# First FFN of a macaron block: the order of its first five row tiles written out for all engines

## The chip, the cores and the metric

The kernel runs on one core of one Trainium2 chip. The metric is the device time of one execution in microseconds; the time before is a median of three runs. The engines are PE (TensorE: matmuls, and PEld for its weight loads), DVE (VectorE), ACT (ScalarE), POOL (GpSimd) and SP (SyncE, here only a queue that issues DMA transfers). Each engine takes its own instructions in order, and semaphores make it wait for the others.

## What is computed

One macaron layer on 2048 rows of 1024 numbers, in float32: half a feed-forward step (FFN), an attention step, half the same FFN again. The FFN is a binary-weight product with eight routed scales:

```python
# reference, cut
xf = x.reshape(-1, H)
routing = softmax(xf @ gate_w.T, axis=1)              # 8 experts
in_scale = routing @ in_channel_scale
out_scale = routing @ out_channel_scale
ffn = xf * in_scale @ sign(weight).T * out_scale + bias
...
x = x + 0.5 * ffn(layernorm(x))
x = x + attn(layernorm(x))        # convolution, 16 heads in blocks of 128, two projections
x = x + 0.5 * ffn(layernorm(x))
```

## The kernel before

The rows are cut into 16 tiles of 128. The program has four stages: the first FFN (to about 198 us of the profiled execution), the convolution, attention, and the second FFN. The change touches the first FFN, and the shared class `Ffn` and function `normalize` that the second also uses.

One tile t of the FFN passes these steps, each a method of `Ffn`. `norm` (line 184) takes the row's mean and variance on DVE (two `bn_stats`, line 155, and line 159), the reciprocal root on POOL (162) and applies them, on ACT (170) or, with `on_vector`, on DVE (166). `transpose` (193) turns the result with eight PE transposes into `xnT`, copied out in two halves. `gate` (203) makes the logits of eight experts, `route` (218) their softmax (the exponential on ACT, the rest on DVE), as a high and a low float32r part; `turn` (236) transposes it. `scale` (243) multiplies the small tables by it: the input scale multiplies `xnT` on DVE (261), the product is cast to float32r `yh` (263, on ACT or DVE) and the rest `yl` is found by POOL (264). `out_scale` (267) makes `osc`, through ACT. `main` (278) is the product of the two terms with the signs `sw`: eight chunks c of the inner dimension, two column halves h, two terms, 32 matmuls of 128x512 a tile (286). Then DVE multiplies a half by `osc` (295) and adds it to the row in place (296). `add_bias` (190) adds half the bias to the row by an accumulating DMA on POOL's queue.

After the FFN, `norm_x2` and `transpose_x2` (388, 395, called as `after` and `between`) store the row, normalise it for the attention step, transpose it into a window and, every third tile, run a transform on DVE (434 to 440).

PSUM has four kinds of banks of two each: `mm` (main products), `acc`, `tr`, `sm`. Rows live in a ring of eight buffers (`xring`), the raw weight rows in six others (`cwp`).

What sets the order: the framework keeps a dependency for each buffer and orders the instructions of each engine by a planner's estimates. Inside `with tc.manual_schedule()` (line 671) it keeps the written order. There stands `begin` (596), which loads the rows and weights, makes the constants and brings tiles 0 and 1 to their products, with the sign steps `sign(c)` on ACT between, and ends with tile 0's product:

```python
        ffn.norm(0)
        ffn.norm(1, on_vector=True)
        ffn.transpose(0)
        ffn.transpose(1, nc.vector.tensor_copy)
...
        def third():
            ffn.transpose(2, nc.vector.tensor_copy)
            ffn.norm(3, on_vector=True)
            ffn.add_bias(3)

        ffn.main(0, 0, 1, between=third)
```

Everything behind is ordered by the planner, along `run` (319), where iteration t holds gate t+2, scale t+1, the first half of product t with route t+2 in its middle, transpose t+3, `between` t-2, norm and bias t+4, the second half with turn t+2 in its middle, and `after` t-1. `pin` and `keep_in_program_order` hold single instructions in program order; the five loads of convolution and attention constants (673) are such, on POOL's queue.

Of the kernel before, what the change touches and what calls it, by code (L numbers as in the profile page):

```python
# [9 lines left out]
F32 = mybir.dt.float32  # L10
F32R = mybir.dt.float32r
DRAM = bass.MemoryType.DRAM
AF = mybir.ActivationFunctionType
# [4 lines left out]
P = 128  # L18
# [6 lines left out]
def kernel(  # L25
# [102 lines left out]
    def table_loads(tmp):  # L128

        raw = tmp[:, 0, 0:NB]  # L130
        for n, src in enumerate((ics, ocs)):
            for h in range(NH2):
                nc.gpsimd.dma_start(
                    out=raw[ts(2 * n + h, QC), :],
                    in_=src[:, ts(h, NB)].unsqueeze(0).broadcast_to([4, E, NB]),
                )
        return raw
# [13 lines left out]
    def normalize(dst, src, name, pinned=False, on_vector=False):  # L151

        stats = small.tile([P, NH2, 6], F32, name=f"st_{name}", tag="stats")
        for h in range(NH2):
            ins = nc.vector.bn_stats(out=stats[:, h, :], in_=src[:, ts(h, NB)])  # L155
            if pinned:
                pin(ins)
        mv = small.tile([P, 2], F32, name=f"mv_{name}", tag="mv")
        nc.vector.bn_aggr(out=mv, in_=stats)
        rstd = small.tile([P, 1], F32, name=f"rs_{name}", tag="rstd")  # L160
        nc.vector.tensor_scalar(rstd, mv[:, 1:2], EPS, None, ALU.add)
        nc.gpsimd.tensor_tensor(rstd, rstd, nhalf, ALU.pow)
        if on_vector:
            for h in range(on_vector):
                cols = ts(h, D // on_vector)
                nc.vector.tensor_scalar(dst[:, cols], src[:, cols], mv[:, 0:1], rstd, ALU.subtract, ALU.mult)
            return
        shift = small.tile([P, 1], F32, name=f"sh_{name}", tag="shift")
        nc.gpsimd.tensor_scalar(shift, mv[:, 0:1], rstd, -1.0, ALU.mult, ALU.mult)
        nc.scalar.activation(dst, src, AF.Identity, bias=shift, scale=rstd)  # L170

    class Ffn:
# [6 lines left out]
        def __init__(self, name, sw, work, xnp, first, end, row, ahead, after, between, beside):  # L179
            self.name, self.sw, self.work, self.xnp, self.first, self.end = name, sw, work, xnp, first, end  # L180
            self.row, self.ahead, self.after, self.between, self.beside = row, ahead, after, between, beside
            self.xns, self.xnTs, self.lgps, self.routs, self.rTs, self.oscs, self.ys = ({} for _ in range(7))

        def norm(self, t, pinned=False, on_vector=False):
            for n in range(t, min(t + 2, self.end)):
                self.ahead(n)
            self.xns[t] = self.xnp.tile([P, D], F32, name=f"xn_{self.name}_{t}", tag="xn")
            normalize(self.xns[t], self.row(t), f"{self.name}_{t}", pinned, on_vector)
# [4 lines left out]
        def transpose(self, t, copy=nc.scalar.copy):  # L193
            xn = self.xns.pop(t)
            xnT = self.work.tile([P, DC, P], F32, name=f"xnT_{self.name}_{t}", tag="xnT", bufs=3)
            for h in range(DC // 4):
                tr = bank("tr", [P, 4, P], f"tr_{self.name}_{t}_{h}")
                for c in range(4):
                    nc.tensor.transpose(tr[:, c, :], xn[:, ts(4 * h + c, P)], ident)  # L199
                copy(xnT[:, 4 * h : 4 * h + 4, :], tr)  # L200
            self.xnTs[t] = xnT
# [41 lines left out]
        def scale(self, t, copy=nc.scalar.copy, out=False):  # L243

            xnT, rT = self.xnTs.pop(t), self.rTs[t]
            yhl = self.work.tile([P, 2, DC, P], F32R, name=f"y_{self.name}_{t}", tag="y")
            scs = [bank("tr", [P, 4, P], f"is_{self.name}_{t}_{h}") for h in range(NH2)]
            for c in range(4):
                for h, sc in enumerate(scs):
                    nc.tensor.matmul(  # L250
                        sc[:, c, :],
                        lhsT=tables[ts(h, QC), ts(c, P)],
                        rhs=rT[ts(h, QC), :],
                        start=True,
                        stop=True,
                    )
            if out:
                self.out_scale(t)
            for h, sc in enumerate(scs):
                y = xnT[:, 4 * h : 4 * h + 4, :]  # L260
                nc.vector.tensor_tensor(y, y, sc, ALU.mult)
                yh, yl = (yhl[:, n, 4 * h : 4 * h + 4, :] for n in range(2))
                copy(yh, y)  # L263
                nc.gpsimd.tensor_tensor(yl, y, yh.bitcast(F32), ALU.subtract)  # L264
            self.ys[t] = yhl
# [12 lines left out]
        def main(self, t, *halves, between=None, at=DC - 2):  # L278
            y, osc, xrow = self.ys[t], self.oscs[t], self.row(t)
            pms = {h: bank("mm", [P, NB], f"pm_{self.name}_{t}_{h}") for h in halves}  # L280
            for c in range(DC):
                if between and c == at:
                    between()
                for h, pm in pms.items():
                    for n in range(2):
                        nc.tensor.matmul(  # L286
                            pm,
                            lhsT=y[:, n, c, :],
                            rhs=self.sw[:, c, ts(h, NB)],
                            start=(c == 0 and n == 0),  # L290
                            stop=(c == DC - 1 and n == 1),
                        )
            for h, pm in pms.items():
                o, xt = osc[:, ts(h, NB)], xrow[:, ts(h, NB)]
                nc.vector.tensor_tensor(pm, pm, o, ALU.mult)  # L295
                nc.vector.tensor_tensor(xt, xt, pm, ALU.add)  # L296
            if NH2 - 1 in pms:
                del self.ys[t], self.oscs[t]

        def fill(self):  # L300
# [8 lines left out]
                lambda: self.scale(a, out=True),  # L309
# [9 lines left out]
        def run(self):  # L319

            for t in range(self.first, self.end):
                self.on(self.gate, t + 2)
                if t + 1 in self.ys:
                    self.out_scale(t + 1)
                elif t + 1 < self.end:
                    self.scale(t + 1, out=True)
                route, turn = (lambda stage=stage: self.on(stage, t + 2) for stage in (self.route, self.turn))
                begun = t not in self.ys  # L330
                if begun:
                    route()
                else:
                    self.main(t, 0, between=route, at=DC // 2)
                self.on(self.transpose, t + 3)
                self.on(self.between, t - 2)
                self.on(self.norm, t + 4, t == self.first)
                self.on(self.add_bias, t + 4)
                if begun:
                    turn()  # L340
                else:
                    self.main(t, 1, between=turn, at=DC // 2)
                self.on(self.after, t - 1)
                self.beside(t)
# [251 lines left out]
    def begin(ffn, work):  # L596
# [5 lines left out]
        def load_raw(c):  # L602
            raws[c] = cwp.tile([P, D], F32, name=f"raw_{c}", tag="cw")
            nc.sync.dma_start(out=raws[c], in_=weight_t[ts(c, P), :])
# [13 lines left out]
        load_x(1)  # L618
        for c in range(6):
            load_raw(c)  # L620
        load_x(2)
        raw = table_loads(tmp)
# [5 lines left out]
        ffn.norm(0)  # L628
        ffn.norm(1, on_vector=True)
        ffn.transpose(0)  # L630
        ffn.transpose(1, nc.vector.tensor_copy)
        for h in range(NH2):
            hb = bank("acc", [P, NB], f"hb_{h}")
            nc.tensor.matmul(hb, lhsT=halves, rhs=brow[:, ts(h, NB)], start=True, stop=True)
            nc.vector.tensor_copy(hbias[:, ts(h, NB)], hb)
        ffn.add_bias(0)
        ffn.add_bias(1)
        ffn.gate(0)
        nc.scalar.copy(upper, raw)
        ffn.route(0)  # L640
        table_terms(raw, upper)
        ffn.gate(1)
        sign(0)
        load_raw(6)
        ffn.turn(0)
        ffn.route(1)
        sign(1)
        load_raw(7)
        load_x(3)
        ffn.scale(0)  # L650
        ffn.turn(1)
        sign(2, 3)
        ffn.scale(1, nc.vector.tensor_copy)
        sign(4, 5)
        ffn.norm(2, on_vector=True)
        ffn.add_bias(2)
        sign(6)
        ffn.out_scale(0)
        sign(7)

        def third():
            ffn.transpose(2, nc.vector.tensor_copy)
            ffn.norm(3, on_vector=True)
            ffn.add_bias(3)

        ffn.main(0, 0, 1, between=third)

    with ExitStack() as ph:
# [6 lines left out]
        ffn.run()  # L675
# [267 lines left out]
    ffn.run()  # L943
# [56 lines left out]
```

## Time and profile before

| | |
|---|---|
| median of three runs | 997.54 us (995.36 to 998.24) |
| the profiled execution's own time | 995.0 us |
| its span, first to last instruction | 992.9 us |
| PE busy in the span | 957.5 us, 96% |
| DVE, ACT, POOL busy | 653.7, 407.7, 256.4 us |
| first FFN: last addition to a row | starts at 198.1 us |
| first matmul of the convolution | 207.0 us |

Times in views are microseconds from the span's start. In a row of a timeline there stand the start, the length, the engine, the line, the operation, what it writes and reads, and how often it ran in a row; a bracket tells how long the engine was idle before it and what released it. Ends of matmuls are modelled, and records of neighbouring instructions overlap a little, so the distance from start to start is the better price of one. The granted clock is TensorE's, 1.00 for full speed.

### The profile page before, as it was taken

How to read it: one execution, taken by the hardware profiler on the slowest of the kernel's cores; microseconds unless marked ns; L12 is line 12 of the kernel's file. 1: busy time of each engine (PE TensorE's matmuls, PEld its weight loads, DVE VectorE, ACT ScalarE, POOL GpSimd, SP SyncE). 2: the span in 40 equal slices, each digit the busy share in tenths (PEclk: the TensorE clock that was granted, in tenths of full speed). 3: DMA queues.
4: the chain of work that ended last, by engine and by line, in shares of the span. 5: the costliest groups of instructions: out<-in, count | busy, mean ns of one | idle time of the engine just before them, and what ended most of it. 6: DMA issues, size and time to landing. Idle time of an engine off the chain costs nothing.

```text
span 992.9 us, 13803 instructions
## 1 busy us (share of the span) xinstructions
PE 957.5 (96%) x5036; PEld 622.8 (63%) x5036; DVE 653.7 (66%) x1231; ACT 407.7 (41%) x1113; POOL 256.4 (26%) x327
## 2 busy tenths in 40 slices
PE   5999999979999999999999999999999999899997
PEld 4778888746666666655555455545554556677776
DVE  5878887798795665637656465546555656777664
ACT  4476765401011111125546244536442653545440
POOL 4455543310011111003313120212022312534321
PEclk8999999989999999999999999999999999999999
DMA  9766554698787764326030430053004217655421
GB/s 271 208 180 195 157 171 153 229 362 300 279 257 178 202 174 123 96 101 228 18 111 1 168 109 1 0 196 102 1 1 170 44 36 209 161 162 158 110 79 64
DMA packets 37252, 143.08 MB, mean 144 GB/s; under 512 B 4345, under 2 KB 5369, under 8 KB 34754
## 3 DMA queue, kind: packets, MB, share of 16 engines
q1 hardware_dynamic: 27616, 101.35, 28.0%
q0 software_dynamic: 8544, 29.64, 15.7%
q10 hardware_dynamic: 1026, 11.22, 2.9%
q8 instruction: 40, 0.66, 0.3%
q14 instruction: 26, 0.21, 0.1%
HBM read 84.37 MB, written 41.04 MB: 126 GB/s over the span
## 4 chain that ended last, share of the span: by engine, by line
PE 47%; issue 26%; DVE 11%; DMA 7%; POOL 6%; ACT 1%; SPq 0%; POOLq 0%; DVEq 0%; ACTq 0%
PE pm_f L286 18%; PE cv L515 16%; POOL xr L774 3%; PE tr_f L199 2%; PE pp L908 2%; DMA xl<-win 2%; POOL p L830 2%; PE acc L889 1%; PE lgp_f L207 1%; PE is_f L250 1%; DVE st_f L155 1%; DMA g<-in_conv_w_dram 1%; PE pq L797 1%; DMA pw_sb<-in_proj_w_dram 1%; DMA xf<-x 1%
## 5 line engine op out<-in xcount | busy, mean ns | idle before, releaser
L286 PE MATMUL pm_f<-sw,y_f 128*128 128x512 f32 x1024 | 266.6, 408 | 0.2 <-DVE x L296 0.2
L286 PEld LDWEIGHTS pm_f<-sw,y_f 128*128 128x128 f32 x1024 | 186.8, 191 | 40.9 <-DVE x L296 0.4
L515 PE MATMUL cv<-v,u 128*128 128x342 f32 x576 | 166.3, 450 | 1.1 <-DVE u L506 1.1
L515 PEld LDWEIGHTS cv<-v,u 128*128 128x128 f32 x576 | 109.0, 189 | 58.2 <-ACT m L521 1.6
L830 POOL TENSOR_SCALAR_AFFINE_SELECT p<-p 128x512 f32<-128x512 f32 x64 | 40.0, 654 | 285.9 <-ACT p L828 285.9
L843 ACT ACTIVATE p<-p,anm 128x128 f32<-128x128 f32 x256 | 99.0, 388 | 17.5 <-DVE anm L840 17.5
L264 POOL TENSOR_TENSOR y_f<-xnT_f,y_f 128x512 fp32r<-128x512 f32 x64 | 81.3, 1288 | 70.0 <-ACT y_f L263 69.2
L521 ACT ACTIVATE m<-cv 128x342 f32<-128x342 f32 x42 | 19.0, 456 | 165.8 <-PE cv L515 148.6
L828 ACT COPY p<-sc 128x512 f32<-128x512 f32 x64 | 34.3, 587 | 111.2 <-PE sc L818 111.1
L840 DVE TENSOR_REDUCE anm<-p 128x4 f32<-128x512 f32 x64 | 40.9, 681 | 49.9 <-POOL p L830 49.9
L889 PE MATMUL acc<-oT,wo_sb 128*128 128x512 f32 x128 | 66.9, 615 | 0.5 <-DVE oT L881 0.5
L515 PE MATMUL cv<-v,g 128*128 128x342 f32 x192 | 56.9, 459 | 4.7 <-DVE v L440 4.7
L295 DVE TENSOR_TENSOR pm_f<-pm_f,os_f 128x512 f32<-128x512 f32 x64 | 44.3, 692 | 25.8 <-PE pm_f L286 25.6
L797 PE MATMUL pq<-qkv,wq_sb 128*128 128x512 f32 x128 | 61.0, 596 | 0.0
L797 PE MATMUL pq<-qkv,wk_sb 128*128 128x512 f32 x128 | 60.1, 592 | 0.0
L908 PE MATMUL pp<-pw_sb,o2T 128*128 128x512 f32 x128 | 57.6, 600 | 0.5 <-DVE xr L916 0.3
L781 PE MATMUL pv<-wv_sb,qkv 128*128 128x512 f32 x128 | 56.1, 592 | 0.0
L515 PEld LDWEIGHTS cv<-v,g 128*128 128x128 f32 x192 | 37.0, 194 | 24.3 <-DVE v L440 4.9
L506 DVE SCALAR_TENSOR_TENSOR u<-g,u 128x1024 f32<-128x1024 f32 x18 | 22.0, 1223 | 40.3 <-issue 30.7
L200 ACT COPY xnT_f<-tr_f 128x512 f32<-128x512 f32 x60 | 32.5, 589 | 37.7 <-PE tr_f L199 37.7
L843 ACT ACTIVATION_READ_ACCUMULATOR p<-p,anm 128x1 f32 x256 | 47.9, 187 | 0.0
L851 DVE TENSOR_TENSOR p<-p,asum 128x512 f32<-128x512 f32 x64 | 45.6, 712 | 2.2
(143 smaller groups left out, 1482.4 us busy)
## 6 DMA issues: line engine op xcount, KB each, us to landing
g<-in_conv_w_dram SPq DMA_DIRECT2D x28, 512.0 KB, 5.3
u<-in_conv_w_dram POOLq DMA_DIRECT2D x24, 512.0 KB, 6.3
xl<-win ACTq DMA_DIRECT2D x7, 1560.0 KB, 10.9
win<-xw SPq DMA_DIRECT2D x6, 1560.0 KB, 6.0
x<-in_x_dram SPq DMA_DIRECT2D x16, 512.0 KB, 4.6
raw<-in_weight_t_dram SPq DMA_DIRECT2D x16, 512.0 KB, 6.9
x<-hbias POOLq DMA_DIRECT2D x16, 512.0 KB, 5.8
x<-x SPq DMA_DIRECT2D x16, 512.0 KB, 5.2
```

Source lines behind the costliest of these rows:

```text
L264: nc.gpsimd.tensor_tensor(yl, y, yh.bitcast(F32), ALU.subtract)
L286: nc.tensor.matmul(pm, lhsT=y[:, n, c, :], rhs=self.sw[:, c, ts(h, NB)], start=(c == 0 and n == 0), stop=(c == DC - 1 and n == 1),)
L295: nc.vector.tensor_tensor(pm, pm, o, ALU.mult)
L515: nc.tensor.matmul(acc, lhsT=uk[:, c, :], rhs=V[k][:, c, :], start=(c == 0), stop=(c == DC - 1))
L781: nc.tensor.matmul(pv, lhsT=qkvs[g][2][:, c, ts(b, P)], rhs=wv_sb[:, c, ts(half, NB)], start=(c == 0), stop=(c == WC - 1),)
L797: nc.tensor.matmul(pq, lhsT=w_sb[:, c, ts(hp, P)], rhs=qkvs[g][n][:, c, :], start=(c == 0), stop=(c == WC - 1),)
L830: nc.gpsimd.affine_select(out=p, in_=p, pattern=[[0, BPG], [-1, P]], compare_op=ALU.is_ge, fill=NEG_INF, base=0, channel_multiplier=1,)
L840: nc.vector.tensor_reduce(nmax, p, AX.X, ALU.max, negate=True)
L843: nc.scalar.activation(p[:, b, :], p[:, b, :], AF.Exp, bias=nmax[:, b : b + 1], accum_out=asum[:, b : b + 1],)
L851: nc.vector.tensor_tensor(p, p, asum.unsqueeze(2).broadcast_to([P, BPG, P]), ALU.mult)
L889: nc.tensor.matmul(accs[g][m], lhsT=wo_sb[:, hp, ts(m, P)], rhs=oT, start=(hp == 0), stop=(hp == NHP - 1),)
L908: nc.tensor.matmul(pp, lhsT=o2T[:, m, ts(b, P)], rhs=pw_sb[:, m, ts(h, NB)], start=(m == 0), stop=(m == WC - 1),)
```

## The change

The written order now covers the first five tiles with all engines, and `run` begins at tile 5. In particular:

- The table loads go through ACT's DMA queue instead of POOL's, ahead of the weight rows in the written order.
- Weight rows 6 and 7 go to two buffers of the row ring and are asked for directly behind the others.
- `normalize` is cut into a class `Norm` with separate steps; tiles 0 and 1 are normalised by DVE in halves, tiles 2 and 3 by ACT.
- The bias copies move from DVE to ACT and ahead of the first norm; the tables' conversion on ACT (`upper`) too.
- `scale` is cut into `in_scale`, `multiply`, `split`, `out_scale`; in the written part casts and low terms are assigned to engines piece by piece, with the eight sign steps in between.
- `main` takes a table `beside` of steps to be written before matmul pair (c, h), and evicts a half directly after its last matmul; `apart` tells from which c the halves go one after the other.

```diff
@@ table_loads
-                nc.gpsimd.dma_start(
+                nc.scalar.dma_start(
@@ Norm
+        def by_vector(self, parts, which):
+            for h in which:
+                cols = ts(h, D // parts)
+                nc.vector.tensor_scalar(
+                    self.dst[:, cols], self.src[:, cols], self.mv[:, 0:1], self.rstd, ALU.subtract, ALU.mult
+                )
...
@@ Ffn
+        def split(self, t, h, copy=nc.scalar.copy, low=nc.gpsimd):
+            y = self.xnTs[t][:, 4 * h : 4 * h + 4, :]
+            yh, yl = self.y_terms(t, h)
+            copy(yh, y)
+            low.tensor_tensor(yl, y, yh.bitcast(F32), ALU.subtract)
...
+        def main(self, t, *halves, beside=None, apart=DC):
...
+            turns = [(c, h) for c in range(apart) for h in pms] + [(c, h) for h in pms for c in range(apart, DC)]
+            for c, h in turns:
+                beside.pop((c, h), lambda: None)()
...
@@ run
-                self.on(self.norm, t + 4, t == self.first)
+                self.on(self.norm, t + 4)
@@ begin
+            pl, tag = (cwp, "cw") if c < 6 else (xring, "x1")
...
         load_x(1)
+        raw = table_loads(tmp)
         for c in range(6):
             load_raw(c)
         load_x(2)
-        raw = table_loads(tmp)
+        load_raw(6)
+        load_raw(7)
+        load_x(3)
...
+            nc.scalar.copy(hbias[:, ts(h, NB)], hb)
+        nc.scalar.copy(upper, raw)
+        norms = [Norm(*ffn.begin_norm(t)) for t in range(2)]
+        norms[0].sums(0)
+        norms[0].sums(1)
+        norms[0].factor()
+        norms[1].sums(0)
+        for h in range(NH2):
+            norms[0].by_vector(2, (h,))
+            ffn.transpose(0, h)
+        norms[1].sums(1)
+        norms[1].factor()
+        ffn.gate(0)
+        table_terms(raw, upper)
+        norms[1].by_vector(2, (0, 1))
+        sign(0)
+        ffn.route(0)
+        ffn.transpose(1, 0)
+        sign(1)
+        ffn.transpose(1, 1, copy=nc.vector.tensor_copy)
+        ffn.turn(0)
         ffn.add_bias(0)
+        ffn.in_scale(0, "acc")
         ffn.gate(1)
+        ffn.multiply(0, 0)
+        sign(2)
+        ffn.split(0, 0, low=nc.vector)
+        ffn.multiply(0, 1)
+        ffn.split(0, 1)
         ffn.route(1)
+        sign(3, 4)
+        def scale_both():
+            ffn.out_scale(0)
+            ffn.in_scale(1)
+            ffn.multiply(1, 0)
+            sign(5)
+            ffn.split(1, 0, nc.vector.tensor_copy)
+            ffn.multiply(1, 1)
+            sign(6, 7)
+            ffn.split(1, 1, nc.vector.tensor_copy)
+            ffn.add_bias(1)
+        def next_rows():
+            ffn.out_scale(1)
+            ffn.norm(2)
+            ffn.add_bias(2)
+        def begin_third():
+            ffn.transpose(2)
+            ffn.norm(3)
+            ffn.add_bias(3)
+        ffn.main(
+            0, 0, 1,
+            beside={(2, 0): then((ffn.turn, 1)), (3, 0): scale_both, (5, 0): next_rows, (7, 1): begin_third},
+            apart=DC - 2,
+        )
+        ffn.main(1, 0, beside={(3, 0): then((ffn.gate, 2)), (6, 0): then((ffn.route, 2))})
+        ffn.transpose(3)
+        ffn.main(
+            1, 1,
+            beside={
+                (1, 1): then((ffn.turn, 2)),
+                (3, 1): then((ffn.scale, 2), (norm, 4), (plus, 4)),
+                (5, 1): then((ffn.gate, 3)),
+                (7, 1): then((ffn.route, 3)),
+            },
+        )
+        ffn.main(2, 0, beside={(2, 0): then((ffn.turn, 3), (ffn.after, 0)), (5, 0): then((ffn.scale, 3))})
...
+        ffn.after(3)
@@ after begin
-        ffn.run()
+        ffn.run(5)
@@ second FFN
-    ffn.run()
+    ffn.run(0)
```

In the part left out of `begin`, tiles 2 to 4 go on in the same manner: norms 5 to 8, gates and routes to 6, scales to 5, transposes to 7, `after` 0 to 3 and `between` 0 to 2 stand beside their products. The five constant loads on POOL's queue still stand behind `begin`.

## The prediction

> **What bounds the kernel now.** I read the page's head and slices first, then the busy time by stage, then the timelines of the engines over the first 90 us, because the change touches only the first feed-forward block (FFN) and mainly its first five row tiles.
>
> ```profile
> span 992.9 us, 13803 instructions
> PE 957.5 (96%) x5036; PEld 622.8 (63%) x5036; DVE 653.7 (66%) x1231; ACT 407.7 (41%) x1113; POOL 256.4 (26%) x327
> PE   5999999979999999999999999999999999899997
> PEclk8999999989999999999999999999999999999999
> ```
>
> PE is busy 96% of the span. The first slice (24.8 us) is at 5 tenths: that is the place where PE time is lost that this change can reach. To see how much, I cut the first 116 us at the starts of the tiles' main products (windows; columns: length, then busy time and count for PE, PEld, DVE, ACT, POOL, then PE clock, DMA share, GB/s).
>
> ```profile
> 0.00:22.00 22.00, 11.79 (x84) 8.53 (x84) 12.21 (x33) 9.37 (x17) 8.27 (x22) 0.85 0.91 274
> 22.00:35.70 13.70, 12.62 (x70) 9.67 (x68) 10.52 (x20) 8.06 (x13) 7.10 (x9) 0.87 0.95 311
> 35.70:49.35 13.65, 13.49 (x97) 9.87 (x97) 12.21 (x34) 6.83 (x16) 7.60 (x12) 0.87 0.54 118
> 49.35:84.00 34.65, 33.11 (x234) 26.39 (x232) 27.76 (x65) 24.11 (x51) 19.21 (x28) 1.00 0.61 167
> 84.00:116.40 32.40, 32.40 (x234) 26.41 (x232) 27.49 (x64) 21.96 (x47) 16.20 (x24) 1.00 0.65 197
> ```
>
> The last row is the settled loop: three tiles in 32.4 us, 10.8 us each, PE never idle. So the loss is 22.0 us ahead of tile 0's products, then tiles of 13.6, 13.6 and 13.0 us. The landmark for everything below is the start of tile 5's products, from where old and new code are the same. PE's timeline gives the starts of tiles 0, 1, 2 and 5:
>
> ```profile
> 22.07 7.37 PE L286 MATMUL pm_f<-sw,y_f 128*128 128x512 f32 x24
> 35.71 3.91 PE L286 MATMUL pm_f<-sw,y_f 128*128 128x512 f32 x9 [0.17 <-DVE x L296]
> 49.35 2.12 PE L286 MATMUL pm_f<-sw,y_f 128*128 128x512 f32 x8
> 83.94 2.11 PE L286 MATMUL pm_f<-sw,y_f 128*128 128x512 f32 x8
> ```
>
> In the second row 9 matmuls take 3.91 us, 0.43 each; in the settled chain of waits 32 take 2.04+1.95+1.83+1.85 = 7.67 us, 0.24 each. The clock by the microsecond says why:
>
> ```profile
> 24.00:25.00 1.00, 1.00 (x4) 0.50 0.97 361
> 25.00:26.00 1.00, 1.00 (x4) 0.72 1.02 418
> 35.00:36.00 1.00, 0.82 (x6) 0.90 0.09 20
> 36.00:37.00 1.00, 1.00 (x3) 0.50 1.03 197
> ```
>
> PE started its first products at half clock and fell back to it at 35.9, after 3.6 us (32.1 to 35.7) without a main product.
>
> **The change, part by part.** I walk the new order with durations of these timelines, each instruction starting when its engine and its inputs are free, 0.1 us per hand-over. Unit rows at half clock: four transposes 0.91 (16 in 3.65), a gate 1.08, a main matmul 0.43; at full clock 0.44, 0.57, 0.24.
>
> *Up to tile 0's gate.* Old: gate at 14.01, because PE first did both tiles' transposes (to 12.1) and the two bias products (12.10 to 14.0), which now run at 3.8 to 5.7, where PE is idle. New: statistics 4.5 to 5.75 (old 4.36; I add 0.15 for the table loads beside them), reciprocal root to 6.85, two half normalisations by DVE of 0.45 (half of 0.81), 6.95 to 7.85, transposes 7.5 to 9.3, the second ACT copy to 10.0, gate at 10.1. ACT must first convert the tables (0.62), and all its later copies queue behind that. By the old queue the tables landed 7.1 to 9.1 us after issue; a plain 512 KB row load beside them took 4.6. Issued by ACT at 1.6 to 2.7, where it idled until 3.89, they land between 6.2 and 11.8. Up to 8 it costs nothing (nor can it gain, since ACT has nothing else to do), at the far end 3.5 us. A row load is the nearest row for a transfer of the same kind of queue, so I take nothing and keep 3.5.
>
> *Gate to products of tile 0.* Old 8.06 us (14.01 to 22.07). New: gate to 11.2, its copy 11.45, logits 11.9, then the exponential waits for sign 0 (1.05, written ahead of it) to 12.5; reciprocal and two products to 13.7, turn 14.25, rT behind one DVE copy at 14.65, input scale 14.8 to 15.9, first multiply to 16.5. ACT is then held: it waits for gate 1's result (17.1), and sign 2 follows, so the cast yh runs 18.4 to 19.0. DVE's low term waits for that and ends at 19.8; queued behind it are the second multiply (to 20.4) and all of tile 1's routing, which turn 1 on PE waits for. Products start at 19.85, 2.2 us earlier than 22.07.
>
> *Tile 0's products.* Eight at 0.43: to 23.3. Tile 1's routing (exponential behind yh at 21.1, end 22.2) is ready for the turn. Four more, still partly slow: 25.0. Both scale groups 0.9, eight products to 27.9, out-scale 0.4, four more to 29.3. Signs 5, 6, 7 follow the two osc products on ACT and end at 27.7, 28.7, 29.7, just in time; three more pairs end at 30.8. Then PE meets tile 2's transposes, written ahead of the last pair. Their row comes late: DVE multiplies and casts tile 1 to 28.8, statistics to 30.3, POOL works through two low terms (1.3 each) and a bias DMA (0.9) before its power at 31.1 to 31.9, ACT normalises 32.0 to 33.2 (1.24). PE waits 2.5 us; then transposes and the last pair, and tile 1 starts at 34.7 (old 35.71).
>
> *Does the clock fall in that wait?* The gap without main products is 30.8 to 34.2, 3.4 us. The row above fell after a gap of 3.6. [...] By the row taken plainly the fall costs half of 3.4 us, 1.7[...]. [...] I take 0 and keep 1.7 for the range.
>
> *Tiles 1 to 4.* Tile 1: 7.67 products, 0.87 transposes, two gates 1.14, scale 0.6, small ones 0.3: 10.6 (old 13.64), so tile 2 starts at 45.4 instead of 49.35. Tiles 2 to 4 are three periods of 10.81 plus what the old code had done by its tile 2 and the new has not: one gate, scale, transposes and turn, 0.57+0.6+0.87+0.1 = 2.1. That is 34.6, so tile 5 starts at 80.0. Against 83.94: **3.9 us earlier**.
>
> *Edits that I put at nothing.* Weight rows 6 and 7 in row buffers no longer wait for signs 0 and 1 (old issue 17.75); their signs are now last on ACT anyway. They hold two of eight row buffers, so row 6 is loaded only at tile 5's norm, some 7 us ahead of use against 4.6 to 6.5 of loading; if late, DVE waits with evictions behind it. The five convolution constants on POOL's queue (0.55 us of issue each, 35.2 to 38.2) move behind the written part, near 80, where POOL is half idle (16.2 of 32.4) and tile 6's low terms have a tile's time; uncovered they cost 2.8. Bias adds queue on POOL between low terms and powers and are in the walk. In the second FFN one norm is no longer pinned: half a microsecond either way, from one statistics pair of 1.2.
>
> The sum against the profiled execution: 995.0 - 3.9 = 991.1. It stands 2.5 under the runs' median 997.54; the same 3.9 from that gives **993.6**.
>
> **Rivals.**
>
> *A, as walked (0.45): 993.6*, its own range 992 to 995.5 (the clock falls: 995.3).
>
> *B, more (0.25): 989.4.* The denser start brings PE to full clock before tile 0's products (12 slow ones save 2.3, of which signs leave about 1.7), and the norm of tile 2 comes in time (2.5): 3.9+4.2 = 8.1. For it: the old trace ran gates at 14.01 in 0.65 for 16, full clock. Against: from 15 to 25 it was at half again.
>
> *C, nothing is left (0.16): 997.5.* The gain is absorbed behind the first FFN, because transfers there wait for bandwidth (DMA 1.01 in 200 to 220), or tables land late. Against: PE's wait at 201 to 207 is for DVE (4.67 us, line 440), which moves along.
>
> *D, slower (0.14): 1001.* DVE becomes the bound of tiles 2 to 4. Written work there: eight norms of 1.4, three multiply pairs of 1.2, seven evictions of 1.45, routings 3.65, the window transform 2.4, together 31.0 us in 34.6. Old: 27.76 in 34.65, with 6.9 idle. A written order lets no later instruction pass a waiting one. From 7.5 us of waits on, the whole gain is gone; with 11 (the old 6.9 and six more like the 0.66 us that DVE stood before line 222's maximum at 15.46, waiting for the logits) the stretch takes 42.0, 7.4 more, minus 3.9: slower by 3.5. Against: the settled loop hides the same waits at 85% busy, and the last eviction and norm (2.9) may spill past the landmark.
>
> **How the numbers follow.** About 0.3%, 3 us, is what a measurement can tell from no change: faster means under 994.5. B and 0.31 of A's 0.45 lie there: 0.56. C and the rest of A: 0.30. D: 0.14. The range 987.5 to 999.0 reaches from beyond B's 989.4, by the scatter of the runs (995.36 to 998.24), to past C, and leaves out most of D and little else.
>
> **What would show it.** Right: tile 0's gate near 10, its products near 19.9 behind a DVE low term, a wait of 2 to 3 us ahead of tile 2's transposes, tile 2 at 45, tile 5 at 80, and an unchanged distance from there to the end. Wrong: the table conversion on ACT after 9; half clock past 36; x loads that release statistics; DVE over 90% busy in 45 to 80 with PE waiting for evictions; or a changed length behind tile 5.

## The result, and the profile after

The changed kernel takes 1028.56 us (median of five runs, 1026.24 to 1030.23) beside 997.75 for the kernel before, measured beside it: a ratio of 1.0306, 95% interval 1.0286 to 1.0327. It is slower by 31 us where 4 us of gain were forecast. The profiled execution of the changed kernel took 1029.2 us, that of the kernel before 995.0, 2.8 under its median here; so the stages below add up to some 3 us more than the medians differ by. The page's head and its slices of PE and clock:

```profile
span 1027.0 us, 13814 instructions
...
PE   5976899997999999999999999999999999899997
...
PEclk9998899998999999999999999999999999999999
```

Slices of 25.7 us: PE, which had stood at 9 tenths from the second slice on, now shows 9, 7, 6, 8 in the second to fifth, up to 128 us, and the clock an 8 in the fourth and fifth. The rest looks as before. Cut at the starts of tiles 0 to 4, 6, 8 and 14 (where one run of matmuls spans two tiles, the cut is found by counting; columns as in the forecast):

```profile
0.00:25.31 25.31, 13.13 (x73) 8.29 (x73) 9.79 (x28) 9.04 (x16) 3.28 (x12) 1.00 0.93 315
25.31:40.60 15.29, 13.01 (x53) 8.93 (x54) 10.26 (x21) 9.55 (x15) 6.62 (x8) 1.00 0.22 48
40.60:56.60 16.00, 12.12 (x88) 8.87 (x88) 6.93 (x17) 7.24 (x15) 5.77 (x8) 0.96 0.66 164
56.60:70.70 14.10, 12.60 (x79) 9.22 (x78) 8.08 (x18) 6.91 (x15) 5.21 (x9) 0.93 0.42 113
70.70:91.00 20.30, 14.01 (x79) 10.57 (x78) 8.67 (x22) 7.56 (x18) 5.10 (x8) 0.83 0.42 104
91.00:125.62 34.62, 28.54 (x190) 20.59 (x188) 21.72 (x51) 15.94 (x32) 14.40 (x24) 0.90 0.35 92
125.62:151.82 26.20, 23.71 (x157) 18.71 (x155) 22.98 (x55) 18.03 (x36) 14.73 (x23) 0.93 0.77 221
151.82:216.23 64.41, 63.88 (x440) 51.56 (x438) 50.22 (x111) 39.25 (x88) 26.55 (x39) 1.00 0.50 157
```

The last row is the settled loop, 64.4 us for six tiles where the kernel before has 64.2 (116.40 to 180.62). So all the loss lies ahead of 152 us, but not all of it in the five written tiles: 4.6 us of it fall in tiles 6 and 7, which the planner orders. Against the kernel before: 3.2 us up to tile 0's products (22.07 in the kernel before), 1.7 in tile 0, 2.4 in tile 1, 1.1 in tile 2, 9.5 in tile 3, 13.0 in tiles 4 and 5 together (34.62 against 21.62), 4.6 in tiles 6 and 7 (26.20 against 21.65), 0.2 in the last row: 35.6 in all. Behind the FFN 1.5 came back, so that the spans differ by 34.1. No engine is the bound in these stages: in 70.7 to 91.0 PE is busy 69%, DVE 43%, ACT 37%, POOL 25%, and still it is the worst of them.

Whom did PE wait for in the first 120 us? (Waits: engine and line that waited, engine and line waited for; us in total, times, longest.)

```profile
PE lgp_f L231 <- ACT xnT_f L223: 15.6, 4, 6.1
...
ACT tables_upper L663 <- DMA tables_raw<-in_ocs_dram: 5.6, 1, 5.6
...
PE lg_f L244 <- ACT lgs_f L239: 4.6, 3, 3.9
```

Once, at the start, ACT waited for the tables. PE's long waits are for copies that ACT makes out of PSUM (xnT, lgs): short work, 0.27 to 0.6 us. So the question is what ACT was doing. Its timeline around the longest, 77.7 to 83.8:

```profile
75.83 1.24 ACT L178 ACTIVATE xn_f<-x,sh_f,rs_f 128x1024 f32<-128x1024 f32 x1 [5.08 <-POOL sh_f L177]
76.98 1.06 ACT L311 ACTIVATE os_f<-po_f 128x512 f32<-128x512 f32 x2
77.93 1.13 ACT L291 CAST y_f<-xnT_f 128x512 fp32r<-128x512 f32 x2
82.03 1.24 ACT L178 ACTIVATE x2n<-x,sh_x,rs_x 128x1024 f32<-128x1024 f32 x1 [2.97 <-POOL sh_x L177]
83.18 1.05 ACT L223 COPY xnT_f<-tr_f 128x512 f32<-128x512 f32 x2
```

And PE in the same stretch:

```profile
76.54 1.17 PE L324 MATMUL pm_f<-sw,y_f 128*128 128x512 f32 x4
83.80 1.14 PE L231 MATMUL lgp_f<-xnT_f,gate_sb 128*32 128x128 f32 x16 [6.09 <-ACT xnT_f L223]
84.87 2.08 PE L324 MATMUL pm_f<-sw,y_f 128*128 128x512 f32 x4
```

The transposed tile lies in PSUM from about 76.6 on. ACT could copy it at 79, but the next instruction in its queue is the normalisation x2n of another row, for which POOL has not yet made the shift; ACT stands for 2.97 us, normalises, and only then copies. Ahead of that it had stood 5.08 us in the same manner, before xn, with the steps that make the next tile's `osc` and `yh` queued behind. PE waits 6.09 us and comes back at half clock: four matmuls in 2.08 us beside 1.17 ahead of the wait, with a granted clock of 0.50 from 83 to 89.

### The profile page after: what moved, and what is told of

Read it like the earlier page. It is cut to its first block, busy times and chain, and to the rows that moved or that the text cites. A ratio compares the mean times of both kernels' runs of the same rounds, so it can differ in the third digit from the quotient of the medians.

```text
span 1027.0 us, 13814 instructions
## 1 busy us (share of the span) xinstructions
PE 970.9 (95%) x5036; PEld 627.5 (61%) x5036; DVE 650.7 (63%) x1228; ACT 412.1 (40%) x1119; POOL 253.3 (25%) x323
## 3 DMA queue, kind: packets, MB, share of 16 engines
q1 hardware_dynamic: 27616, 101.35, 27.6%
## 4 chain that ended last, share of the span: by engine, by line
PE 43%; issue 32%; POOL 9%; DMA 8%; DVE 6%; ACT 2%; POOLq 0%; SPq 0%; ACTq 0%; DVEq 0%
PE cv L542 18%; PE pm_f L324 16%; POOL xr L891 3%; DMA xf<-x 2%; PE tr_f L222 2%; POOL p L947 2%; POOL y_f L292 2%; PE lgp_f L231 1%; PE pp L1025 1%; DMA x<-xr 1%; DMA x<-in_x_dram 1%; PE is_f L272 1%; DMA tables_raw<-in_ocs_dram 1%; DMA out_dram<-xf 1%; PE tr L433 1%
## 5 line engine op out<-in xcount | busy, mean ns | idle before, releaser
L324 PE MATMUL pm_f<-sw,y_f 128*128 128x512 f32 x1024 | 275.2, 415 | 2.2 <-ACT y_f L291 1.9
L324 PEld LDWEIGHTS pm_f<-sw,y_f 128*128 128x128 f32 x1024 | 188.0, 194 | 45.3 <-issue 2.6
```

Of the source, the lines that this page charges most:

```text
L324: nc.tensor.matmul(pms[h], lhsT=y[:, n, c, :], rhs=self.sw[:, c, ts(h, NB)], start=(c == 0 and n == 0), stop=(c == DC - 1 and n == 1),)
```

## Experiments

Each was timed beside the kernel before on the same chip (997.2 us in the first set of four, 997.5 in the second, 996.4 in the third). Since these differ by a microsecond, I take what an edit is worth from the ratios: 0.001 is 1.0 us, the changed kernel stands at 1.0306, and the intervals are about 1.2 to 3 us either way. My first theory was W: DVE's statistics go through POOL, where the power and shift queue behind two low terms of 1.3 us, and ACT's copies queue behind the normalisation that waits for it. The rivals: L, the late tables with everything else their echo; S, the seam behind tile 4, where the written order ends and the planner's begins.

**Tables back on POOL's queue.**

```diff
-                nc.scalar.dma_start(
+                nc.gpsimd.dma_start(      # in table_loads
```

> Changed kernel with the table loads back on POOL's queue, all else as it is. Theory W (written order of tiles 1 to 4 is the cause: DVE statistics go through POOL's queue behind two low terms, and ACT's copies queue behind the normalisation that waits for it): the tables land near 10 instead of 15.2, tile 0's products start near 20 instead of 25.3, the end comes about 5 us earlier, 1023.5. Rival L (the late tables are the cause, all later waits are their echo): at least 20 us earlier, 1008 or less. Rival S (the seam behind tile 4, with the five constants and the row ring): 1028 or 5 less, as W.

Measured 1023.56 us (ratio 1.0270, 1.0255 to 1.0285): 3.6 faster than the changed kernel, near what W had, and S too. L falls: the tables are an eighth of the loss. They landed at 12.2, still too late for an ACT queue in which their conversion stands first; products of tile 0 start at 22.19, not at 20.

**Norms ahead of the scale.**

```diff
-                (3, 1): then((ffn.scale, 2), (norm, 4), (plus, 4)),
+                (3, 1): then((norm, 4), (plus, 4), (ffn.scale, 2)),
...
-                (4, 0): then((ffn.scale, 4), (ffn.after, 1)),
+                (4, 0): then((ffn.after, 1), (ffn.scale, 4)),
```

(Norm 5 and `after` 2 likewise.)

> Changed kernel in which, in the written tiles 1 to 4, each norm or x2 norm that stands directly behind a scale stands ahead of it, so that its power and shift on POOL come before the low terms. W: the waits of PE for xnT and lgs (3.9, 1.4, 6.1, 2.7 us in this stretch) shrink to a third, 12 to 18 us earlier, about 1013. L: unchanged, 1028. S: unchanged, 1028.

Measured 1029.29 us (1.0325, 1.0308 to 1.0341): 1.9 slower if anything, no gain. W falls in this form; S had expected just that. POOL's low terms are no longer in front of the power, but the wait has only moved. PE's waits in this kernel:

```profile
PE lgp_f L231 <- ACT xnT_f L223: 11.4, 3, 5.7
PE pm_f L324 <- ACT y_f L291: 3.6, 2, 2.7
...
PE lg_f L244 <- ACT lgs_f L239: 3.0, 3, 2.2
```

Now `osc` and the casts to `yh` stand behind the waiting normalisation, and the copies behind those.

**Tiles 1 to 4 left to the planner**, with their text unchanged.

```diff
         with tc.manual_schedule():
-            begin(ffn, work)
+            then = begin(ffn, work)       # ends with tile 0's products
+        go_on(ffn, then)                  # the same text for tiles 1 to 4
```

> Changed kernel in which only the part up to tile 0's products is in written order; the text of tiles 1 to 4 is the same but the planner orders it. W: tile 5 starts some 15 to 20 us earlier, 1006 to 1012 in all, the rest being the late tables. L: unchanged within 3 us, 1028. S: the planner has no seam left, about 1010 too, but then the second kernel of this set changes nothing.

Measured 1004.32 us (1.0076, 1.0061 to 1.0091): 23 faster. The same instructions, moved only within their queues, are worth three quarters of the loss. This doesn't tell W from S, which had expected about 1010: the planner removes the seam as well. What is left against the kernel before is 7.6 us.

**Low terms on DVE.**

```diff
-        def scale(self, t):
+        def scale(self, t, low=nc.gpsimd):
...
-                self.split(t, h)
+                self.split(t, h, low=low)   # written tiles: low=nc.vector
```

> Changed kernel in which the low terms of tiles 2 to 5 are computed by DVE (0.69 us for one in the changed kernel's trace) instead of POOL (1.3). W: POOL's powers no longer queue behind 2.5 us of low terms; DVE takes 1.4 us more a tile and waits for the casts: 6 to 12 us earlier, about 1020. L and S: unchanged, 1028; if DVE were the bound of these tiles (the forecast's rival D), slower, 1033.

Measured 1038.51 us (1.0431, 1.0402 to 1.0460): 12.5 slower, where W expected 8 faster. That speaks against POOL as the place a second time. S, which expected no change, doesn't explain it. The forecast's rival D had it slower, but DVE's load isn't the reason: it is busy 37.1 of the 74 us from 36 to 110. DVE's multiplies now stand behind low terms that wait for ACT's casts, 12.3 us in all between 36 and 125. The transposes wait for DVE's multiplies (L286) up to 3.55 us here. The kernel has one more in-order wait, on another engine.

So I formed theory A: what costs is an instruction at the head of ACT's queue that waits for others, whichever work of others that is. Its rival P: the row itself is late.

**Statistics where they are, normalisation on ACT later.**

```diff
-                (3, 1): then((ffn.scale, 2), (norm, 4), (plus, 4)),
-                (5, 1): then((ffn.gate, 3)),
+                (3, 1): then((ffn.scale, 2), (stats, 4)),
+                (5, 1): then((ffn.gate, 3), (apply, 4), (plus, 4)),
...
-                (4, 0): then((ffn.scale, 4), (ffn.after, 1)),
+                (4, 0): then((ffn.scale, 4), (after_stats, 1)),
...
-                (2, 1): then((ffn.gate, 5)),
+                (2, 1): then((ffn.gate, 5), (apply, 6), (plus, 6), (after_apply, 1)),
```

(Norms 5 to 7 and the x2 norms of rows 0 and 2 likewise. Bias additions, which need the normalised row, and the x2 transposes `between` 1 and 2 are written later with them.)

> Changed kernel; in the written tiles 1 to 4 statistics, power and shift of norms 4 to 7 and of x2 norms 0 to 2 stay where they are, only the normalisation on ACT that waits for them is written later, behind the copies of the next transpose or gate. Theory A (ACT's queue: copies and casts that PE needs stand behind a normalisation that waits for DVE and POOL; that is why moving the whole norm ahead of the scale only moved the wait to osc and yh): PE's waits for xnT and lgs in tiles 1 to 4 go, 10 to 16 us earlier, about 1015. Rival P (what is late is the row itself, the chain eviction, statistics, power, normalisation, whatever queue it stands in): no gain, 1028 plus or minus 2.

Measured 1015.62 us (1.0174, 1.0157 to 1.0191): 13.2 faster, A's 10 to 16; P falls. POOL's low terms are still ahead of the power; only ACT no longer stands and waits for it. ACT's waits in 40 to 110 us, first of the changed kernel, then of this one:

```profile
ACT xn_f L178 <- POOL sh_f L177: 16.2, 5, 5.7
ACT x2n L178 <- POOL sh_x L177: 11.4, 3, 5.4
```

```profile
ACT os_f L317 <- PE is_f L278: 6.8, 2, 5.2
ACT os_f L317 <- PE po_f L315: 5.6, 2, 3.2
ACT xn_f L180 <- POOL sh_f L177: 5.2, 4, 2.9
...
ACT x2n L180 <- POOL sh_x L177: 1.0, 1, 1.0
```

27.6 us of standing before a normalisation have become 6.2, and what ACT waits for most is now PE. But S stays beside A. Counted in their traces, tile 4's products start 17.8 us later than in the kernel before (73.13) with the changed kernel, and 8.7 later here; tiles 4 to 7, 43.2 us in the kernel before, take 60.9 and 56.5. So most of this gain lies ahead of tile 4, and 13 us of loss stay in tiles 4 to 7. With tiles 1 to 4 planned these take 45.7, of which 2.4 us are work of PE that the kernel before does ahead of tile 4.

**Constants ahead of the written part**: the loop of five `nc.gpsimd.dma_start` moved from behind `begin` to ahead of it.

> Changed kernel with the five constant loads written ahead of the written part instead of behind it. In its trace they stand at 120.7 to 123.4 on POOL between the two low terms of a tile. Theory S (they are on the path there): 2 to 3 us earlier, 1026. If they only filled a wait: 1028.

Measured 1027.81 us (1.0299, 1.0270 to 1.0329): 0.7 less than the changed kernel, inside the scatter. Whether they cost anything isn't settled; the interval reaches from 3.6 us of gain to 2.3 of loss. In the profiled execution, the fastest of four, the convolution starts 2.7 us earlier than in the changed kernel's.

**Tables and planner together.** (Edits of the first and third experiment.)

> Tables back on POOL's queue and tiles 1 to 4 left to the planner, the two single gains together. If they add (5.0 and 24.2 of 31.4 us): 999.3, within 0.3% of the kernel before. If the late tables only cost where the written order follows: about 1003.

Measured 1001.57 us (1.0032, 1.0019 to 1.0044): 4.4 faster than the planned tiles alone, beside 3.6 for the tables in the changed kernel. The two add, within the scatter, so the tables' price isn't an effect of the written order of tiles 1 to 4.

**And the start mended.**

```diff
-        nc.scalar.copy(upper, raw)          # ahead of tile 0's copies
...
         ffn.gate(0)
-        table_terms(raw, upper)
         norms[1].by_vector(2, (0, 1))
-        sign(0)
+        nc.scalar.copy(upper, raw)
         ffn.route(0)
         ffn.transpose(1, 0)
+        sign(0)
         sign(1)
...
+        table_terms(raw, upper)
         ffn.turn(0)
...
-        sign(2)
         ffn.split(0, 0, low=nc.vector)
+        sign(2)
```

> As the kernel before it in this set, and in the written start the tables' conversion stands behind tile 0's logits instead of ahead of its copies, and signs 0 and 2 behind the exponential and the first casts. With the tables' landing near 12 no copy waits for it: tile 0's gate near 10.5, products near 19, 3 us earlier than with the tables alone: 996, one or two us faster than the kernel before. If the half clock and tile 2's late transposes set the pace instead: 999, unchanged against its neighbour.

Measured 997.69 us (1.0008, 0.9995 to 1.0021): equal to the kernel before. Three steps, 23, 4.4 and 2.4 us, account for all but 0.8 of the loss. Tile 0's gate is at 10.59 and its products at 19.96, 2 us ahead of the old, but nothing is left of that in the time.

**New start, old loop**: the mended start up to tile 0's products, then the old `run` from tile 0.

> The written start with tables on POOL's queue and the later table conversion, up to tile 0's products, then the old loop from tile 1 on, ordered by the planner. Theory A, that the text of tiles 1 to 4 is worth nothing even to the planner: tile 0's products at 20 against 22.1 and nothing lost afterwards, 2 us faster than the kernel before, 995.5. If the start's gain is given back where tile 2's transposes wait inside tile 0's products: 997.5.

Measured 996.08 us (0.9997, 0.9984 to 1.0010). No gain, the second of the two expectations. Products of tile 0 start at 19.91, 2.2 us earlier than in the kernel before, and the convolution at 207.00 against 207.03. The lead is gone by tile 1, whose products start at 36.22 against 35.71. PE stands 2.29 us before tile 2's transposes, which are written inside tile 0's products and wait for the row's normalisation; how far that wait and how far the loop's own order takes the rest was not separated.

**The written order, mended.** Five tiles in written order, with the tables and start of the experiments above, and each normalisation of tiles 4 to 7 and x2 0 to 2 behind the next exponential:

```diff
-        ffn.main(2, 0, beside={(2, 0): then((ffn.turn, 3), (ffn.after, 0)), (5, 0): then((ffn.scale, 3))})
+        ffn.main(2, 0, beside={(1, 0): then((apply, 4), (plus, 4)), (2, 0): then((ffn.turn, 3), (after_stats, 0)), (5, 0): then((ffn.scale, 3))})
         ffn.transpose(4)
+        after_apply(0)
...
-                (4, 1): then((ffn.route, 5), (ffn.between, 1)),
+                (4, 1): then((ffn.route, 5)),
+                (5, 1): then((apply, 6), (plus, 6), (after_apply, 1)),
```

> The written order of five tiles kept, with tables on POOL's queue, the later table conversion, and every normalisation of tiles 4 to 7 and x2 0 to 2 on ACT written behind the next exponential, the x2 transposes half a tile later. Theory A: 13 us of the deferred normalisation, 8 to 9 of the start, and some 3 to 5 for the exponential that still stood behind it: 1003. If the rest belongs to the seam or to row loads: 1007 or more.

Measured 1002.34 us (1.0070, 1.0057 to 1.0084), as A had it: 23.6 of the 30.6 us are back with the order still written by hand. PE's waits in its first 130 us:

```profile
PE tr_f L228 <- ACT xn_f L180: 5.6, 2, 3.3
...
PE is_f L278 <- DVE rs_f L165: 2.4, 1, 2.4
...
PE lg_f L250 <- ACT lgs_f L245: 0.8, 2, 0.4
```

The wait for xnT is gone from the list, and up to tile 4 so is the whole loss: its products start at 68.85, 4.3 us ahead of the kernel before, though with some 3 us of transposes, a gate and a scale still to do. (The forecast's 45.4 for tile 2, 45.3 by its own terms, and two periods of 10.81 make 67.0.) Tile 8's start at 123.88, 7.5 behind. What is left therefore lies in tiles 4 to 7, at the seam, where PE stands twice:

```profile
91.18 1.97 PE L228 MATMUL tr_f<-ident,xn_f 128*128 128x128 f32 x8 [3.34 <-ACT xn_f L180]
112.42 0.33 PE L278 MATMUL is_f<-rT_f,tables 32*128 32x128 f32 x2 [2.37 <-DVE rs_f L165]
```

After the first PE runs at half speed again (transposes in 1.97 us instead of 1.04; the granted clock was 0.95 in the mean of 60 to 95). Before the second, DVE's statistics had themselves waited 2.2 us for a row load, issued at 104.55 and landed at 111.48. Neither wait was removed by itself, so the cause of the other 7 us stays open.

**Tables on SP's queue**, behind the first two rows and ahead of the weight rows: `nc.sync.dma_start` in `table_loads`.

> Changed kernel with the four table loads on SP's queue, behind the first two rows and ahead of the weight rows. If the tables are late because four small transfers of a second queue share the engines with 3 MB of weight rows issued at the same time: they land by 8 here, tile 0's gate starts near 11 and the end is 5 to 7 us earlier, 1022. If the loads are slow by their own shape (rows of 2 KB read four times): still 13 to 15, 1028.

Measured 1021.16 us (1.0253, 1.0237 to 1.0269): 5.3 faster than the changed kernel, as expected if the tables land early. The first lines of PE show the start as it was forecast:

```profile
10.32 1.18 PE L231 MATMUL lgp_f<-xnT_f,gate_sb 128*32 128x128 f32 x16 [0.15 <-ACT xnT_f L223]
...
19.23 4.08 PE L324 MATMUL pm_f<-sw,y_f 128*128 128x512 f32 x8 [0.87 <-ACT y_f L291]
```

ACT waits 0.3 us for the tables, which have landed by 9.2. So their shape isn't slow. What decides is how they are issued beside the weight rows; whether by the queue or by the place ahead of them, this edit, which changes both, doesn't tell.

**The old kernel with the tables on ACT's queue.**

> The kernel before with one edit, the table loads on ACT's queue ahead of the weight rows. Its conversion stands behind tile 0's logits, at 14.9. If the tables land at 15.2 as in the changed kernel: routing of tile 0 waits under 1 us, 998. If ACT's issuing and the delayed weight issue matter: 1000.

Measured 996.36 us (1.0005, 0.9994 to 1.0017): nothing. In its profiled execution the products of tile 0 start at 24.68, 2.6 us later than in the kernel before, and the convolution at 209.51, 2.5 later, so there the delay is not taken up. But that execution (999.82 us) lies above its own median, and executions of this kernel ranged from 993.9 to 1000.6. Why the medians don't differ stays open.

## Why the prediction was wrong

**What held.** The reading of the loss ahead of tile 5 in the kernel before, and the settled loop (10.8 us a tile, 64.4 for six). The walk of the start: gate at 10.1 and products at 19.85 were forecast, and with tables in time the chip shows 10.32 and 19.23. The wait before tile 2's transposes: 2.5 forecast, 2.28 in the changed kernel. Of the forecast's signs of being wrong, four came: the conversion after 9 (15.28), half clock past 36 (0.50 from 83 to 89), statistics released by a row load (1.3 us at 137.85), and a changed length behind tile 5. DVE over 90% busy did not come.

**The tables' landing** was mis-sized. I put it between 6.2 and 11.8 and took a row load of 4.6 as the nearest row; they landed at 15.2, 13.6 us after the first issue. The forecast had "at the far end 3.5 us" and took nothing; it is worth 3.6 us (POOL's queue) to 5.3 (SP's queue, where they are in time). ACT was to issue them between 1.6 and 2.7 and took until 5.25. The row load that I took was issued ahead of the weight rows; these were issued beside six of them. The nearest row was weight rows themselves, in the kernel before 6.9 to 12.5 us to landing.

**The step that failed is "Tiles 1 to 4: 10.6 ... three periods of 10.81 ... 34.6".** Up to tile 1 I walked the new order on all engines. From there I added up PE's work and took the settled period for granted, as if the written order were the planner's. I named the rule that breaks it, "a written order lets no later instruction pass a waiting one", but gave it to DVE, by its load: rival D. DVE was busy 47% of 36 to 110 us. The queue that mattered was ACT's, less loaded still, at 43% (31.5 of 74): eight normalisations stood at its head for 27.6 us, with casts and PSUM copies behind. In the changed kernel's trace it shows in tile 1, right behind the end of the walk; rows of POOL, then of ACT, then of PE:

```profile
50.35 2.50 POOL L292 TENSOR_TENSOR y_f<-xnT_f,y_f 128x512 fp32r<-128x512 f32 x2 [6.50 <-ACT y_f L291]
52.82 0.56 POOL L166 TENSOR_TENSOR rs_f<-rs_f,nhalf 128x1 f32<-128x1 f32 x1
...
49.64 1.14 ACT L291 CAST y_f<-xnT_f 128x512 fp32r<-128x512 f32 x2
53.77 1.24 ACT L178 ACTIVATE xn_f<-x,sh_f,rs_f 128x1024 f32<-128x1024 f32 x1 [2.99 <-POOL sh_f L177]
54.92 0.24 ACT L239 COPY lgs_f<-lgp_f 128x128 f32<-128x128 f32 x1
...
55.22 0.59 PE L244 MATMUL lg_f<-fold,lgs_f 128*128 128x8 f32 x2 [3.88 <-ACT lgs_f L239]
```

Scale 2 ends on ACT at 50.8. Norm 4 behind it waits for POOL's two low terms, power and shift until 53.8, gate 3's copy stands behind it until 54.9, and PE is 3.9 us late. D's size (7.4) was too small as well, because such a wait recurs each tile and some of them bring PE back at half clock (0.50 from 83 to 89, and again from 103.5 to 109.5). With the normalisations moved, the mended order keeps the forecast's pace up to tile 4 within 2 us, which speaks for the walk of PE's work and for this as the step that failed.

**A second step failed with it**: the landmark, "the start of tile 5's products, from where old and new code are the same", with "an unchanged distance from there to the end". The code is the same there; the state that the written part leaves behind is not. Tiles 6 and 7 alone took 4.6 us more than in the kernel before, and in the mended order all that is left lies there and in tiles 4 and 5. No experiment changed the seam alone, but for the constants; what costs it there isn't shown.

**Edits put at nothing.** The constants: 2.8 if uncovered, in the forecast; 0.7 measured, not settled. Weight rows in row buffers and the unpinned norm: no trace of a cost, but neither was tried alone.

**The clock in the wait of 2.3 us.** Both ends that I kept occur. The 1.7 is half of the 3.4 us for which the kernel before had a granted clock of 0.50 (35.8 to 39.2); the 0 that I took was an estimate, which no trace of that kernel shows. After the same wait the first eight matmuls took 2.09 us in the changed kernel, with a granted clock of 1.00 from 36 to 45, and 3.30 with tiles 1 to 4 planned (0.26 and 0.41 each):

```profile
40.12 2.09 PE L324 MATMUL pm_f<-sw,y_f 128*128 128x512 f32 x8
```

```profile
39.03 3.30 PE L324 MATMUL pm_f<-sw,y_f 128*128 128x512 f32 x8
```

Nine of the kernels have this wait, 2.27 to 2.29 us, with eight matmuls behind its transposes. In four profiled executions the eight took 3.26 to 3.37 us, in five 2.09. Four of the nine have the same written order up to there: the changed kernel and norms ahead of the scale took 2.09, low terms on DVE 3.37, normalisation later 3.33. So a wait of this length was followed by half speed in some executions and not in others. Why is not shown, and which of 0 and 1.7 it would be could not have been told from these traces. Nor did the denser start bring full clock to tile 0's first products, as rival B had it: with tables in time (SP's queue) eight of them took 4.08 us.

## What to carry to other kernels

An order written by hand has to be walked on every engine, through every tile that it covers, and what is looked for is not load but an instruction that waits at the head of a queue with others' work behind it: a copy that PE needs belongs ahead of a normalisation that waits for two other engines, even if that engine is half idle (ACT was busy 43% here). When a wait only moves to another place after one instruction is moved, as it did with the norms ahead of the scale, the queue is to be suspected before the work named in the wait. Where a written order ends and a planner's begins, the tiles behind the seam belong to the forecast too. And the landing time of a small transfer is taken from transfers issued under the same load (here 13.6 us, beside weight rows that took 7.2 to 11.9).

## What was not expected of the hardware

DMA issue on one queue went more slowly beside that on another. With the tables on ACT's queue SP needed 7.63 us to issue six weight rows; with them on POOL's queue 3.35, and 3.10 in the kernel before. The first line is of the changed kernel, the second of the one with tables on POOL's queue:

```profile
1.63 7.63 SPq L632 DMA_DIRECT2D raw<-in_weight_t_dram  x6
```

```profile
1.62 3.35 SPq L632 DMA_DIRECT2D raw<-in_weight_t_dram  x6
```

ACT's own last two table issues took 2.16 us together in the first of these kernels, with 0.9 us between them. What the two queues share there, the traces don't show.
